# One attention and mixture kernel on one core: scores and values issued back to back, and the last two tiles interleaved

## The chip, the core and the metric

The kernel runs on one core of a Trainium2 chip. A core has a matrix engine (TensorE, "PE" in the profile; its weight loads are shown apart as "PEld"), VectorE (DVE), ScalarE (ACT), GpSimd (POOL) and SyncE (SP), which issues the transfers (DMAs) here. Each engine works through its own queue in order, and engines wait for one another by semaphores. In this kernel TensorE writes its results to an accumulation memory (PSUM), from which VectorE and ScalarE copy them out. The metric is the time of one execution in microseconds (us), as the median of several runs; lower is better. Beside it stands one profiled execution, whose "span" goes from its first to its last instruction.

## The reference

Two sandwich blocks on 4 sequences of 512 tokens, 1024 wide, all in float32. Attention is causal with 32 heads of 32 columns that share 8 key and value heads; the second block is a dense layer with eight low-rank experts, two of them chosen for each token.

```python
x = x + _layernorm(attn(_layernorm(x), w_qkv, b_qkv, w_o, b_o))
x = x + _layernorm(ffn(_layernorm(x), gate_w, base_w, base_b, lora_A, lora_B))

# attn
qkv = x @ w_qkv.T + b_qkv
...
scores = jnp.einsum('bhqd,bhkd->bhqk', rope(q), rope(k)) / math.sqrt(HEAD_DIM)
attn = jax.nn.softmax(jnp.where(causal, scores, -1e20), axis=-1)
out = jnp.einsum('bhqk,bhkd->bhqd', attn, v)
return out.reshape(bs, seq_len, d_model) @ w_o.T + b_o

# ffn
weights, selected = jax.lax.top_k(x @ gate_w.T, 2)
w_full = jnp.sum(jax.nn.one_hot(selected, E) * jax.nn.softmax(weights)[..., None], axis=2)
low = jnp.einsum('bsd,erd->ebsr', x, lora_A)
return x @ base_w.T + base_b + 2.0 * jnp.einsum('ebsr,eor,bse->bso', low, lora_B, w_full)
```

## The kernel before

The 2048 tokens are 16 tiles of 128. They are worked on in the order of `line`: tiles 0 to 11, then 13, 14, 15, and tile 12 last. Tile t is the i-th of its sequence (i = t mod 4), and its queries see i + 1 blocks of 128 keys. So tile 12, the first of its sequence, has the shortest attention.

For each tile: x is loaded (`load_x`), normalised (`Norm`: statistics on VectorE, the root on GpSimd, the scaling on VectorE) and transposed on TensorE (`transposes`, tiles pt_xn, copied out to T_xn). `project` multiplies it by the query, key and value weights in eight steps of 128 rows (acc_kv, acc_q); `rotated` applies the rotary angles; TensorE turns keys and queries (pt_k, pt_q) into kT and qT.

Attention runs in groups. A group holds one to four of the eight columns of heads in a tile, and four heads ("quadrants") for each column. There are 2, 4, 8 or 8 groups for i = 0, 1, 2, 3: 88 in all. A group's stages:

- `scores`: matmuls that use only 32 rows of the array, four side by side, one for each quadrant (sc, 32*128 in the profile). There is one buffer for sc in PSUM, and four smaller ones for everything else that TensorE writes.
- `softmax`: VectorE adds the causal mask on the diagonal block (L1019) and takes the maxima of all four quadrants (L1029). Then, quadrant by quadrant, ScalarE takes exponentials and sums (L982), VectorE the reciprocals (L991), GpSimd scales (L996): pr.
- `turn`: TensorE transposes a quadrant's pr (pt_p, L1043); VectorE or ScalarE copies it out (prT). pr and prT share eight buffers.
- `values`: matmuls that use only 32 columns of the array (av, L1066, 128*32 in the profile), copied out to aT.

`attention_out` multiplies aT by the output weights (acc_o), adds the bias (L740), normalises, adds into y on GpSimd (`add_half`, L401), and normalises again to w. `ffn` transposes w (pt_h, copied to T_h), multiplies it by the gate and low-rank weights (acc_gl), picks the experts (`gate`), transposes the weighted low part (pt_low), multiplies by the base and low-rank weights (acc_f), normalises, adds into y on GpSimd, and stores the two halves.

The order of all instructions is made by a planner in the program, `Order`, before anything runs. It holds an estimated duration for each operation, a clock for each engine, and Tasks that carry the time at which something is finished. `Order.run` gives each of VectorE, ScalarE, GpSimd and SP the most urgent ready operation; `copy` can go to either of two engines. `Order.tensor` gives TensorE its next step from lanes: the scores, the transposes of each tile, the transposes and values of the groups (all these are "urgent", in that order), and then the dense products. A step that has been ready for SAFE (0.6 us) is taken first, otherwise one that is just ready, and otherwise the planner lets its clock go on. What the planner writes down is each engine's order; the chip then runs at its own pace, with semaphore waits.

A group's scores need the queries, the keys, the exponentials of the group before (which frees sc) and the transposes of the group before that. Its values need all four prT.

Of the kernel before, what the change touches and what calls it, by code (L numbers as in the profile page):

```python
# [16 lines left out]
P = 128  # L17
# [13 lines left out]
FILL = 0.3  # L31
SAFE = 0.6
# [44 lines left out]
class Step:  # L77


    def __init__(self, us, issue, needs=(), bank=False):  # L80
        self.us, self.issue, self.needs = us, issue, list(needs)
        self.bank = bank
        self.done = Task()


class Order:
# [14 lines left out]
    def _go_on(self, chain, task, at):  # L101
        self.at = at
# [74 lines left out]
    def tensor(self, urgent, dense):  # L177


        while any(urgent) or any(dense):  # L180
            self.run(self.now)
            known, safe = [], None
            dense = [lane for lane in dense if lane]
            urgent = [lane for lane in urgent if lane]
            for lane in urgent + sorted(dense, key=lambda lane: lane[0].bank):
                at = self._ready(lane[0])
                if at is not None:
                    known.append((at, lane))
                    if at + SAFE <= self.now:
                        safe = lane  # L190
                        break
            if safe is None:
                lane = next((lane for at, lane in known if at <= self.now), None)
                if lane is None:
                    later = [at for at, _ in known]
                    what = self._next()
                    if what is not None:
                        later.append(max(what[0], self.now + 1e-6))
                    if not later:
                        raise RuntimeError("TensorE's work cannot go on")  # L200
                    self.now = min(later)
                    continue
                safe = lane
            step = safe.pop(0)
            if step.bank:
                heapq.heappop(self.banks.free)
            step.issue()
            self.now += step.us
            step.done.finish(self.now + FILL)
        self.run(float("inf"))  # L210
# [3 lines left out]
def kernel(  # L214
# [130 lines left out]
    class Norm:  # L345
# [6 lines left out]
        def half(self, src, h):  # L352
            if self.stats is None:
                self.stats = small.tile([P, NH, 6], F32, tag="stats", name=f"stats_{self.name}")
            cols = slice(h * 512, (h + 1) * 512)
            yield dve(
                0.69,
                self.urgent,
                lambda: nc.vector.bn_stats(out=self.stats[:, h, :], in_=src()[:, cols]),  # L359
            )  # L360

        def scale(self):
            name = self.name

            def aggr():
                self.mv = small.tile([P, 2], F32, tag="mv", name=f"mv_{name}")
                nc.vector.bn_aggr(out=self.mv, in_=self.stats)

            def eps():
                self.veps = small.tile([P, 1], F32, tag="veps", name=f"veps_{name}")  # L370
                nc.vector.tensor_scalar_add(self.veps, self.mv[:, 1:2], EPS)  # L371

            def root():
                self.rstd = small.tile([P, 1], F32, tag="rstd", name=f"rstd_{name}")
                nc.gpsimd.tensor_tensor(out=self.rstd, in0=self.veps, in1=neg_half, op=ALU.pow)  # L375
# [20 lines left out]
    def add_half(y, z, h, urgent):  # L396
        cols = slice(h * 512, (h + 1) * 512)
        yield pool(
            1.3,
            urgent,  # L400
            lambda: nc.gpsimd.tensor_tensor(  # L401
                out=y()[:, cols], in0=y()[:, cols], in1=z()[:, cols], op=ALU.add
            ),
        )
# [119 lines left out]
    class Job:  # L524


        def __init__(self, tok, name, has_k=True, has_q=True):
            self.tok, self.name, self.has_k, self.has_q = tok, name, has_k, has_q
            self.issued, self.in_x = Task(), Task()
# [13 lines left out]
    def load_x(job):  # L543
# [5 lines left out]
        def issue():  # L549
            job.issued.finish(order.at)  # L550
            job.xn = xpool.tile([P, D], F32, tag="xa", name=f"xa_{job.name}")
            nc.sync.dma_start(out=job.xn, in_=x[job.tok.t * P : (job.tok.t + 1) * P, :])

        yield sp(P * D * 4 / 1024 / RATE, issue)
        yield LANDS
        job.in_x.finish(order.at)
# [16 lines left out]
    def qkv(job, has_k, has_q):  # L573
# [6 lines left out]
        def normed():  # L580
            yield job.in_x
            for h in range(NH):
                yield from norm.half(lambda: job.xn, h)
# [129 lines left out]
    def attention_out(tok):  # L713
# [31 lines left out]
        def sum_half(h):  # L745
            yield from norms[0].apply(w, w, h)
            yield from add_half(lambda: tok.y, w, h, 1)
# [71 lines left out]
    def ffn(tok):  # L819
# [67 lines left out]
        def out_half(h):  # L887
            yield from norm.apply(lambda: tok.w, lambda: tok.w, h)
            yield from add_half(lambda: tok.y, lambda: tok.w, h, 2)
# [55 lines left out]
    class Group:  # L945
        def __init__(self, tok, at, n):
            self.tok, self.seq, self.at, self.n = tok, tok.seq, at, n
            self.kt = at // GROUP
            self.name = f"{tok.t}_{at}"
            self.exps, self.normed = [Task() for _ in range(QUADS)], [Task() for _ in range(QUADS)]  # L950
# [3 lines left out]
    def scores(g):  # L954
# [15 lines left out]
        nmax = small.tile([P, QUADS, GROUP], F32, tag="nmax", name=f"nmax_{g.name}")  # L970
        total = small.tile([P, QUADS, GROUP], F32, tag="total", name=f"total_{g.name}")
        rtot = small.tile([P, QUADS, GROUP], F32, tag="rtot", name=f"rtot_{g.name}")
# [34 lines left out]
        def softmax():  # L1007
# [5 lines left out]
            if not seq.left[g.kt]:  # L1013
                kT_slots.give(order.at)
            diag = sc4[:, :, :, i * P : n]
            yield dve(
                0.15 + g.n * 0.54,
                1,
                lambda: nc.vector.tensor_tensor(  # L1019
                    out=diag,  # L1020
                    in0=diag,
                    in1=cmask.unsqueeze(1).unsqueeze(1).to_broadcast([P, QUADS, g.n, P]),
                    op=ALU.add,
                ),
            )
            yield dve(
                0.15 + g.n * n * 0.0042,
                1,
                lambda: nc.vector.tensor_reduce(  # L1029
                    nmax[:, :, : g.n], sc4, AX.X, ALU.max, negate=True  # L1030
                ),
            )
            for r in range(QUADS):
                start(quadrant(r), order.at)
# [104 lines left out]
    for tok in line:  # L1139
        n = min(GROUP, NQ // (tok.i + 1))  # L1140
        for at in range(0, ND, n):
            g = Group(tok, at, n)
            blocks = n * (tok.i + 1)
            needs = [tok.has_q[g.kt]] + [tok.seq.has_k[i] for i in range(tok.i + 1)]
            if groups:
                needs += groups[-1].exps
            if len(groups) > 1:
                needs += [s.done for s in groups[-2].turned]
            g.scored = Step(0.2 + 0.218 * blocks, partial(scores, g), needs)
            g.turned = [  # L1150
                Step(0.109 * blocks, partial(turn, g, r), [g.normed[r]], bank=True)
                for r in range(QUADS)
            ]
            needs = g.has_prT + [tok.seq.has_v[i] for i in range(tok.i + 1)] + [tok.aT_taken]
            g.valued = Step(0.2 + 0.218 * blocks, partial(values, g), needs, bank=True)
            score_lane.append(g.scored)
            value_lane += g.turned + [g.valued]
            groups.append(g)
# [14 lines left out]
    order.tensor([score_lane, *turn_lanes, value_lane], dense_lanes)  # L1173
# [77 lines left out]
```

## Time and profile before

| | us |
|---|---|
| median of 3 runs (lowest and highest) | 1246.99 (1245.8, 1247.3) |
| the profiled execution | 1245.69 |
| its span | 1243.8 |
| first matmul starts | 7.60 |
| last product on TensorE starts (two passes) | 1233.92 |
| time on the chain that ended last: acc_f, acc_q, acc_o | 20%, 18%, 17% of the span |
| the same: transposes pt_p, scores sc, values av | 12%, 7%, 6% |

How to read it: the profile gives, for each engine, the time in which it was busy, and for each group of instructions the line, the engine, the tiles written and read, the count, the busy time and the mean of one. Float32 products take two passes through the array, so one step of `project` shows as two matmuls. Matmuls overlap in the pipeline, and their ends are modelled; the distance from one start to the next is what they really cost. "idle before" is the time in which the engine did nothing before such instructions, and behind the arrow stands what ended most of it. Granted clock over the span: 0.998.

### The profile page before, as it was taken

Reading aid. Unit: us, or ns where it says so; the run is one execution under the profiler, and the core shown is the slowest. Engines: PE = TensorE matmul, PEld = TensorE weight load, DVE = VectorE, ACT = ScalarE, POOL = GpSimd, SP = SyncE. Lnnn points to the kernel's source line nnn. Section 1 sums busy time; section 2 is a strip of 40 time slices with the busy share of each in tenths; the row PEclk is TensorE's granted clock in tenths of the full one; section 3 lists DMA queues with packets and bytes.
Section 4 is the critical chain, followed back from the end, with each engine's and each line's share of the span. In section 5 each row is a group of like instructions: output and inputs, shape, how many; then the busy total and the mean of one; then the engine's idle time right before and its main releaser. Section 6 shows DMA issues by size and latency. Waiting matters only on the chain.

```text
span 1243.8 us, 19733 instructions
## 1 busy us (share of the span) xinstructions
PE 1221.4 (98%) x7416; PEld 653.2 (53%) x7416; DVE 803.5 (65%) x1655; ACT 428.4 (34%) x1354; POOL 452.2 (36%) x700
## 2 busy tenths in 40 slices
PE   7999999999999999999999999999999999999997
PEld 3555555555555555555545555555555555555543
DVE  3656668666566675776555667677657766757553
ACT  0344344444212443344313323344333333343400
POOL 1343425325332443335242423434324334343332
PEclk9999999999999999999999999999999999999999
DMA  9700001001010100101010101002001010010010
GB/s 353 303 1 18 1 1 52 1 1 52 1 51 1 52 1 17 36 1 34 2 51 1 52 1 52 2 1 69 1 1 51 1 52 1 1 51 1 1 34 34
DMA packets 16205, 44.67 MB, mean 36 GB/s; under 512 B 2160, under 2 KB 3184, under 8 KB 16112
## 3 DMA queue, kind: packets, MB, share of 16 engines
q1 hardware_dynamic: 16112, 43.42, 10.0%
q8 instruction: 59, 0.97, 0.3%
q14 instruction: 34, 0.28, 0.1%
HBM read 35.03 MB, written 8.39 MB: 35 GB/s over the span
## 4 chain that ended last, share of the span: by engine, by line
PE 96%; DVE 1%; issue 1%; POOL 1%; DMA 0%; ACT 0%; POOLq 0%; ACTq 0%
PE acc_f L442 20%; PE acc_q L442 18%; PE acc_o L442 17%; PE pt_p L1043 12%; PE acc_kv L442 9%; PE sc L962 7%; PE av L1066 6%; PE acc_gl L442 3%; PE pt_xn L417 1%; PE pt_h L417 1%; PE pt_q L666 1%; POOL y L401 0%; PE pt_k L635 0%; DVE stats L359 0%; DMA xa<-in_x_dram 0%
## 5 line engine op out<-in xcount | busy, mean ns | idle before, releaser
L996 POOL TENSOR_SCALAR pr<-pr,rtot 128x256 f32<-128x256 f32 (+3 forms) x512 | 280.4, 562 | 377.0 <-DVE rtot L991 324.5
L982 ACT ACTIVATE pr<-sc,nmax 128x256 f32<-128x256 f32 (+3 forms) x512 | 262.9, 533 | 146.7 <-DVE nmax L1029 133.0
L442 PE MATMUL acc_f<-wbase_sb,T_h 128*128 128x512 f32 x512 | 241.0, 598 | 0.0
L442 PE MATMUL acc_o<-wo_sb,aT 128*128 128x512 f32 x512 | 237.8, 598 | 0.4 <-ACT aT L280 0.4
L442 PE MATMUL acc_q<-wqkv_sb,T_xn 128*128 128x512 f32 x480 | 225.3, 597 | 1.0 <-DMA wqkv_sb<-in_w_qkv_dram 0.9
L280 ACT COPY prT<-pt_p 128x512 f32<-128x512 f32 (+1 forms) x189 | 102.2, 549 | 304.5 <-PE pt_p L1043 303.7
L1043 PEld LDWEIGHTS pt_p<-ident,pr 128*128 128x128 f32 x1280 | 148.7, 141 | 108.3 <-issue 81.6
L1029 DVE TENSOR_REDUCE nmax<-sc 128x4 f32<-128x1536 f32 (+3 forms) x88 | 184.2, 2093 | 1.4
L1043 PE MATMUL pt_p<-ident,pr 128*128 128x128 f32 x1280 | 181.2, 275 | 1.1 <-POOL pr L996 1.1
L281 DVE COPY prT<-pt_p 128x512 f32<-128x512 f32 (+1 forms) x163 | 104.4, 641 | 90.8 <-PE pt_p L1043 88.7
L442 PEld LDWEIGHTS acc_o<-wo_sb,aT 128*128 128x128 f32 x512 | 90.6, 190 | 88.8 <-issue 87.6
L442 PEld LDWEIGHTS acc_f<-wbase_sb,T_h 128*128 128x128 f32 x512 | 89.2, 190 | 79.6 <-issue 78.9
L442 PEld LDWEIGHTS acc_q<-wqkv_sb,T_xn 128*128 128x128 f32 x480 | 84.1, 190 | 79.5 <-issue 75.1
L442 PE MATMUL acc_kv<-wqkv_sb,T_xn 128*128 128x512 f32 x256 | 121.6, 601 | 0.6 <-DVE T_xn L281 0.6
L1019 DVE TENSOR_TENSOR sc<-sc,cmask 128x512 f32<-128x512 f32 (+2 forms) x88 | 82.5, 938 | 48.5 <-PE sc L962 47.7
L982 ACT ACTIVATION_READ_ACCUMULATOR pr<-sc,nmax 128x1 f32 x512 | 108.4, 212 | 0.0
L401 POOL TENSOR_TENSOR y<-y,w 128x512 f32<-128x512 f32 x64 | 84.3, 1326 | 64.8 <-DVE w L386 53.3
L375 POOL TENSOR_TENSOR rstd<-veps,neg_half 128x1 f32<-128x1 f32 x64 | 35.3, 553 | 178.1 <-DVE veps L371 153.0
L1066 PEld LDWEIGHTS av<-prT,v 128*32 128x32 f32 x2560 | 65.2, 109 | 63.9 <-issue 34.7
L962 PE MATMUL sc<-kT,qT 32*128 32x384 f32 (+3 forms) x1024 | 93.9, 464 | 0.0
L1066 PE MATMUL av<-prT,v 128*32 128x128 f32 x2560 | 90.0, 276 | 1.0 <-DVE veps L371 0.6
L489 POOL TENSOR_TENSOR raw_q<-raw_q,rope_sb 128x512 f32<-128x512 f32 x32 | 41.0, 1281 | 121.1 <-DVE turn_q L478 104.6
(81 smaller groups left out, 903.7 us busy)
## 6 DMA issues: line engine op xcount, KB each, us to landing
xa<-in_x_dram SPq DMA_DIRECT2D x16, 512.0 KB, 3.5
y<-in_x_dram SPq DMA_DIRECT2D x16, 512.0 KB, 3.6
out_dram<-y SPq DMA_DIRECT2D x32, 256.0 KB, 2.0
wqkv_sb<-in_w_qkv_dram SPq DMA_DIRECT2D x8, 512.0 KB, 9.5
wo_sb<-in_w_o_dram SPq DMA_DIRECT2D x8, 512.0 KB, 8.3
wbase_sb<-in_w_base_dram SPq DMA_DIRECT2D x8, 512.0 KB, 10.4
wqkv_sb<-in_w_qkv_dram SPq DMA_DIRECT2D x8, 256.0 KB, 6.4
bqkv_sb<-in_b_qkv_dram SPq DMA_DIRECT2D x1, 768.0 KB, 7.8
```

The costliest lines, as they stand in the source:

```text
L280: act=(0.15 + n * 0.00085, lambda: nc.scalar.copy(out(), in_())),
L281: dve=(0.15 + n * 0.00105, lambda: nc.vector.tensor_copy(out(), in_())),
L401: lambda: nc.gpsimd.tensor_tensor(out=y()[:, cols], in0=y()[:, cols], in1=z()[:, cols], op=ALU.add),
L442: nc.tensor.matmul(acc[0][:, :n], lhsT=lhsT()[:, c, :] if c < ND else more[0](), rhs=w_sb[:, c, at : at + n] if c < ND else more[1][:, at ...
L489: lambda: nc.gpsimd.tensor_tensor(out=raw3, in0=raw3, in1=cos, op=ALU.mult),
L962: nc.tensor.matmul(sc[:, r, c * n : (c + 1) * n], lhsT=tok.qT[g.kt][rows, (g.at + c) % GROUP, :], rhs=seq.kT[g.kt][rows, :n], start=True, ...
L982: lambda: nc.scalar.activation(pr[:, c * n : (c + 1) * n], sc4[:, r, c, :], AF.Exp, bias=nmax[:, r, c : c + 1], accum_out=total[:, r, c : ...
L996: lambda: nc.gpsimd.tensor_scalar(pr[:, c * n : (c + 1) * n], pr[:, c * n : (c + 1) * n], rtot[:, r, c : c + 1], 1.0, ALU.mult, ALU.mult,),
L1019: lambda: nc.vector.tensor_tensor(out=diag, in0=diag, in1=cmask.unsqueeze(1).unsqueeze(1).to_broadcast([P, QUADS, g.n, P]), op=ALU.add,),
L1029: lambda: nc.vector.tensor_reduce(nmax[:, :, : g.n], sc4, AX.X, ALU.max, negate=True),
L1043: nc.tensor.transpose(pt[:, j, :], g.pr[r][:, j * P : (j + 1) * P], ident)
L1066: nc.tensor.matmul(av[r * HD : (r + 1) * HD, c, :], lhsT=g.seq.v[j][:, head * HD : (head + 1) * HD], rhs=g.prT[r][:, c * (i + 1) + j, :], ...
```

## The change

It has seven parts.

1. *Pairs.* Scores and values are marked `tiled`. When a score step is chosen and the next value step is ready, both are issued together. A score step that is ready is put last if the next value step will come (all it needs but the prT of the group has been given a time) and is not ready yet; a value step is put last likewise if the next score step will come. `soon` names the needs that don't count for "will come": the exponentials of the group before for scores, prT for values.
2. *Costs in the planner.* A tiled step costs 0.4 us (TILING) on top of its work when alone, and 0.55 (PAIRED) for a pair; before it was 0.2 each.
3. *Interleaving.* The groups of the last two tiles (15 and 12) no longer follow tile by tile: tile 12's first group comes before the last two of tile 15.
4. *Maxima in two parts* for the last two tiles: mask and maximum for two quadrants, then for the other two.
5. *The last tile's additions into y* may go to VectorE or GpSimd.
6. *x is loaded in two halves*, and the statistics of a half start when that half is there.
7. *More small buffers*: 4 instead of 2 for a norm's statistics, 3 instead of 2 for the sums of the softmax.

```diff
+TILING = 0.4
+PAIRED = 0.55
...
-    def __init__(self, us, issue, needs=(), bank=False):
-        self.us, self.issue, self.needs = us, issue, list(needs)
-        self.bank = bank
+    def __init__(self, us, issue, needs=(), bank=False, soon=()):
+        self.us, self.issue, self.needs = us, issue, list(needs) + list(soon)
+        self.tiled = False
+        self.bank, self.soon = bank, soon
...
+    def _is_ready(self, step):
+        at = self._ready(step)
+        return at is not None and at <= self.now
+
+    def _comes(self, step):
+
+        return all(t.at is not None for t in step.needs if t not in step.soon)
+
+    def _choice(self, scores, values, lanes):
+
+        later, ready, last = [], [], []
+        score = scores[0] if scores else None
+
+
+        value = values[0] if values and values[0].tiled else None
+        waiting = []
+        if score is not None and value is not None:
+            if self._comes(score):
+                waiting.append(values)
+            if self._comes(value) and not self._is_ready(value):
+                waiting.append(scores)
+        for lane in lanes:
+            at = self._ready(lane[0])
+            if at is None:
+                continue
+            later.append(at)
+            if at <= self.now:
+                if any(lane is w for w in waiting):
+                    last.append(lane)
+                elif at + SAFE <= self.now:
+                    return lane, None
+                else:
+                    ready.append(lane)
+        if ready or last:
+            return (ready + last)[0], None
...
+            steps = [lane.pop(0)]
+            us = steps[0].us + TILING * steps[0].tiled
+            if lane is scores and values and values[0].tiled and self._is_ready(values[0]):
+                steps.append(values.pop(0))
+                us = steps[0].us + steps[1].us + PAIRED
+            for step in steps:
+                self._take(step)
+            self.now += us
...
-                self.stats = small.tile([P, NH, 6], F32, tag="stats", name=f"stats_{self.name}")
+                self.stats = small.tile([P, NH, 6], F32, tag="stats", bufs=4, name=f"stats_{self.name}")
...
-    def add_half(y, z, h, urgent):
+    def add_half(y, z, h, urgent, either=False):
+
         cols = slice(h * 512, (h + 1) * 512)
...
+        def issue(engine):
+            engine.tensor_tensor(out=y()[:, cols], in0=y()[:, cols], in1=z()[:, cols], op=ALU.add)
+
+        on = {"pool": (1.3, partial(issue, nc.gpsimd))}
+        if either:
+            on["dve"] = (0.7, partial(issue, nc.vector))
+        yield Op(urgent, **on)
...
+        for h in range(NH):
+            cols = slice(h * 512, (h + 1) * 512)
+            yield sp(
+                P * 512 * 4 / 1024 / RATE,
+                lambda: nc.sync.dma_start(out=job.xn[:, cols], in_=x[rows, cols]),
+            )
+            start(lands(h), order.at)
+        job.issued.finish(order.at)
...
+            self.parts = 2 if self.tok in line[-2:] else 1
...
+            q = QUADS // g.parts
+            for r0 in range(0, QUADS, q):
+                some = slice(r0, r0 + q)
+                diag = sc4[:, some, :, i * P : n]
+                yield dve(
+                    0.15 + q * g.n * 0.135,
...
+                        nmax[:, some, : g.n], sc4[:, some], AX.X, ALU.max, negate=True
+                    ),
+                )
+                for r in range(r0, r0 + q):
+                    start(quadrant(r), order.at)
...
-            g.scored = Step(0.2 + 0.218 * blocks, partial(scores, g), needs)
...
+        groups += [Group(tok, at, n) for at in range(0, ND, n)]
+
+    *groups, g0, g1 = groups
+    groups.insert(len(groups) - 0, g1)
+    groups.insert(len(groups) - 3, g0)
+    for k, g in enumerate(groups):
...
+        soon = groups[k - 1].exps if k else []
+        if k > 1:
+            needs += [s.done for s in groups[k - 2].turned]
+        g.scored = Step(0.218 * blocks, partial(scores, g), needs, soon=soon)
...
+        needs = [tok.seq.has_v[i] for i in range(tok.i + 1)] + [tok.aT_taken]
+        g.valued = Step(0.218 * blocks, partial(values, g), needs, bank=True, soon=g.has_prT)
+        g.scored.tiled = g.valued.tiled = True
...
-    order.tensor([score_lane, *turn_lanes, value_lane], dense_lanes)
+    order.tensor(score_lane, turn_lanes, value_lane, dense_lanes)
```

## The prediction

> **What bounds the kernel now.** I read the page first: who is busy, and the chain that ended last.
>
> ```profile
> PE 1221.4 (98%) x7416; PEld 653.2 (53%) x7416; DVE 803.5 (65%) x1655; ACT 428.4 (34%) x1354; POOL 452.2 (36%) x700
> ...
> PE 96%; DVE 1%; issue 1%; POOL 1%; DMA 0%; ACT 0%; POOLq 0%; ACTq 0%
> ```
>
> TensorE is the bound nearly everywhere, so an edit pays if it takes time out of TensorE's own row, or a wait out of it. Next, TensorE's timeline over one group (start, length, count; a start is the reliable number):
>
> ```profile
> 1108.77 1.02 PE L442 MATMUL acc_q<-wqkv_sb,T_xn_12q 128*128 128x512 f32 x2
> 1109.72 1.14 PE L962 MATMUL sc<-kT,qT 32*128 32x512 f32 x8
> 1110.79 1.09 PE L1043 MATMUL pt_p<-ident,pr 128*128 128x128 f32 x8
> 1111.72 1.88 PE L442 MATMUL acc_q<-wqkv_sb,T_xn_12q 128*128 128x512 f32 x4
> 1113.54 1.08 PE L1066 MATMUL av<-prT,v 128*32 128x128 f32 x32
> 1114.55 2.84 PE L442 MATMUL acc_q<-wqkv_sb,T_xn_12q 128*128 128x512 f32 x6
> 1117.22 0.60 PE L666 MATMUL pt_q<-ident,raw_q 128*128 128x128 f32 x4
> ```
>
> Elsewhere a full-array pass of 512 columns starts every 0.429 us and a transpose every 0.109 (median start to start in the trace). Here 2 passes should take 0.86 and the scores start after 0.95: going into a tiled form costs 0.09. The last score pass starts 0.517 before the next full-array one, not 0.429: coming out costs 0.09. Then eight transposes take 0.93 and not 0.87, six dense passes 2.67 and not 2.57: the first weight load after a tiled block is not hidden, 0.056 before transposes, 0.104 before dense passes. All 88 score blocks and 88 value blocks of the trace show these values within 0.01.
>
> Summed so, TensorE's row is full-array passes 1013.9, tiled blocks 169.8, 176 entries 16.4, first loads 14.5, waits 12. The waits are the start (about 4), some 2 in the middle, and the end (the bracket gives the idle time and its releaser):
>
> ```profile
> 1144.86 0.66 PE L1043 MATMUL pt_p<-ident,pr 128*128 128x128 f32 x4 [1.08 <-POOL pr L996]
> ...
> 1197.48 1.19 PE L442 MATMUL acc_gl<-wgl_sb,T_h 128*128 128x136 f32 x8 [0.94 <-DVE T_h L281]
> ...
> 1199.90 1.19 PE L442 MATMUL acc_gl<-wgl_sb,T_h 128*128 128x136 f32 x8 [0.78 <-DVE veps L371]
> ```
>
> By starts these are 1.25, 1.1 and 0.94 late; two value blocks (at 1145.4 and 1179.7) take 2.16 and 2.37 where others take 1.01, and 0.2 is unhidden loads: 6.0 in all.
>
> **The change, part by part**, against the profiled execution's 1245.69 us (span 1243.8). The median of the runs shown, 1246.99, is 1.3 higher, which I add at the end.
>
> *Pairing.* In the new TensorE order 68 score blocks are followed at once by a value block and 2 the other way round; in the old order none is. Entries fall from 176 to 106. First loads were 96 before dense passes and 80 before transposes (14.5); now 15 and 91: 15 x 0.104 + 91 x 0.056 = 6.7, so 7.8 less. Changes of form were 352; now 106 in, 106 out and 70 between two tiled forms. The price of the last kind, x, is in no row. From below it is 0 (no drain); from above 0.29, out through the full array and in again (0.09 + 0.09 + 0.104). Every change that the trace has costs 0.088 to 0.094, whatever stands on either side, so I take x = 0.093: 70 fewer changes x 0.093 = 6.5. Sum: -14.3; with x = 0 it is -20.8, with 0.29 -0.5.
>
> The Trainium skill, "TensorEngine Tiling (Array Packing)", Tiling Modes, says that changing the tiling mode, not just the tile, drains the engine. That speaks against x = 0, but gives no price.
>
> *What the pairing delays.* A score step now waits for the next values, so softmax has more TensorE work over it: from a score block to its first transpose the old order has at least 5.85 us of TensorE work (which did not stall), the new one 7.9 or more except at two places at the end. Between two scores the least was 5.3 and is, but for the same places, 8.0. The added cover costs nothing in the middle; were it gone, each stall would be paid in full. One first transpose of a token loses its cover (0.44, the same that cost 0.84 at 112 us in the old run), one stall of 0.78 (at 422) goes. I set the middle to 0.
>
> *The interleaving.* The order is now: tile 15's groups 0 to 5, tile 12's first, tile 15's groups 6 and 7, tile 12's last. Tile 15's output projection needs group 6, which now comes one group later. Between tile 14's last output-projection pass and the transposes of its normalised sum (pt_h) TensorE has three tiled blocks (3.4 with entries), 20 transposes (2.2) and loads (0.2): 5.75 us. The same chain, on VectorE in the old run:
>
> ```profile
> 1134.04 0.69 DVE L740 TENSOR_TENSOR w<-acc_o,bo_sb 128x512 f32<-128x512 f32 x1 [0.17 <-PE acc_o L442]
> ...
> 1143.98 2.29 DVE L1019 TENSOR_TENSOR sc<-sc,cmask 128x2048 f32<-128x2048 f32 x1
> 1146.31 2.29 DVE L1029 TENSOR_REDUCE nmax<-sc 128x16 f32<-128x2048 f32 x1
> ...
> 1151.24 1.00 DVE L386 TENSOR_SCALAR w<-y,mv,rstd 128x512 f32<-128x512 f32 x2 [0.67 <-POOL rstd L375]
> ```
>
> Bias at 1134.0, first half normalised at 1151.8: 17.8 us, then hidden under tile 15's projection. In the new VectorE queue the same operations again have a group's maxima and both mask and maxima of tile 12's first group among them. In two parts these are 1024 columns: mask 1.23 (its 1024 row), maximum 2.29 - 2 x 0.53 = 1.22 (0.53 from the 2048 and 1536 rows). Walked through: bias 0.7, two maxima and a mask 2.9, statistics and reciprocals 1.5, probability copies waiting for transposes 1.8, normalise 0.5, two copies behind the scores 1.8, four halves of mask and maximum 4.9, normalise, add (POOL 1.3) and statistics 2.9, root and normalise 1.2: 18.2, near the row. I take the row: TensorE waits 17.8 + 0.15 (hand-over) - 5.75 = 12.2. Lower bound: the chain with the softmax out of its way took 10.6 (at 1196.1 to 1206.7): 4.8. Upper, by the walk with slips: 16. All that follows on TensorE is late by as much.
>
> A wait of that length also touches the clock. The windows view has
>
> ```profile
> 1239.60:1243.80 4.20, 0.00 (x0) 0.00 (x0) 0.00 (x0) 0.00 (x0) 1.30 (x2) 0.50 0.33 125
> ```
>
> (the 0.50 is the granted clock): half clock 4.7 us after the last matmul. And after the idle start the first eight transposes took 1.71 instead of 0.87 and the first sixteen passes 7.6 instead of 6.9: 1.6 lost. In the new hole I see two idle stretches, near 4 and 8 us, about a value block; one is over 4.7: +1.6 (0 if the clock stays).
>
> The Trainium skill, "TensorE: Matmul & The Clock Gate", Part 1, has the clock halved after one idle window of about 3.4 us; by that both stretches would do it, which would put a further 1.6 on the sum. No run here shows an idle of 4 us followed by work.
>
> *End.* The old end waits go: tile 12's last values have 1.8 us of projection after their transposes, and the gate's products 2.2 and 1.8 after pt_h, where the old waits were about 1.1 after the transposes' end. -6.0. Splitting adds 2 VectorE instructions to each of 10 groups, hidden but for the walk above.
>
> *Tail.* Both last sums go to VectorE (two of 0.7, like the 0.725 row of L494) from GpSimd (2.71). VectorE's four then end at about 1240.0 and not 1240.9: -0.9.
>
> *Start.* x in halves lets the first statistics (0.65) begin before the second half lands, but the fifth query chunk came at 21.8 by DMA and its bytes are the same; only the second token's normalisation gains: -0.5 (0 to -0.65). Twice as many x loads queue on SP; from load to use there is idle SP time in every token. More small buffers only remove waits.
>
> Sum: -14.3 + 12.2 + 1.6 - 6.0 - 0.9 - 0.5 = -7.9: 1237.8, as a median **1239.1**.
>
> **Rivals.** *A, the switch between tiled forms is dear* (slower): at each of the 70 pairs x = 0.29, since the two forms split the array in different directions. For it: no such pair is in the trace. Against: all changes cost the same. -7.9 + 13.8 = +5.9: 1252.9. It decides from x = 0.206 on (7.9 / 70 above 0.093). *B, the hole is short*: the chain runs almost bare, 4.8, and the clock stays: -7.9 - 7.4 - 1.6: 1230.1. For it: maxima in two parts and smaller softmax pieces; against it the queue order. *C, tiled to tiled is free*: x = 0: 1232.6. *D, the pairs are not made*: the order shows 70 of 88, so I give it nothing.
>
> **How the numbers follow.** Forecast 0.55, A 0.16, B 0.15, C 0.14. The forecast's own width is the hole's +-3 and the clock. The range 1231 to 1249 leaves out A's upper part and B's lower. What this kernel's measurement can tell from no change is 0.2%, 2.5 us. Faster: 0.48 of the forecast, B and C, 0.01 of A: 0.78. Same: 0.06 + 0.02 = 0.08. Slower: 0.13 of A, 0.01 of the forecast: 0.14.
>
> **What would show it.** In the new profile: the start of av after the last sc pass (0.52 for 512 columns if x = 0.09, 0.43 if free, 0.7 if dear); a hole of 10 to 14 us before pt_h of tile 14, some 100 us ahead of the end, with transposes of 0.21 after it; no waits over 0.3 behind it; last sums on DVE. Waits in the middle, or a hole of under 6 us, would make the prediction wrong.

## The result, and the profile after

The changed kernel takes 1246.62 us (median of 14 runs, 1245.2 to 1247.96), the kernel before, beside it, 1246.29 (14 runs): ratio 1.0001, 95% interval 0.9993 to 1.001. The forecast gain of 7.9 us did not come. The profiled execution took 1246.57 with a span of 1244.7 (before: 1245.69 and 1243.8), at a granted clock of 0.991 instead of 0.998.

The page first: TensorE's share, the chain that ended last, and two of the costliest groups (busy time and mean ns, then idle time before them and what ended it).

```profile
PE 1212.1 (97%) x7416; PEld 659.6 (53%) x7416; DVE 807.8 (65%) x1678; ACT 430.2 (35%) x1355; POOL 450.6 (36%) x696
...
PE 96%; DVE 2%; ACT 0%; POOL 0%; DMA 0%; issue 0%; POOLq 0%; SPq 0%; ACTq 0%
...
L1103 PE MATMUL pt_p<-ident,pr 128*128 128x128 f32 x1280 | 178.9, 277 | 13.5 <-POOL pr L1053 13.0
L1089 DVE TENSOR_REDUCE nmax<-sc 128x4 f32<-128x1536 f32 (+5 forms) x98 | 185.6, 1894 | 9.7 <-ACT pr L1039 8.7
```

The same two groups on the page of before:

```profile
L1029 DVE TENSOR_REDUCE nmax<-sc 128x4 f32<-128x1536 f32 (+3 forms) x88 | 184.2, 2093 | 1.4
L1043 PE MATMUL pt_p<-ident,pr 128*128 128x128 f32 x1280 | 181.2, 275 | 1.1 <-POOL pr L996 1.1
```

TensorE is less busy than before (1221.4), in a span that is not shorter. New idle time stands ahead of the transposes of probabilities: 13.5 us instead of 1.1, nearly all ended by GpSimd's scaling. And VectorE's maxima now wait for ScalarE's exponentials, which should come after them (9.7 us instead of 1.4). TensorE's timeline shows where (start, length, in brackets the idle time before):

```profile
1108.04 1.14 PE L1019 MATMUL sc<-kT,qT 32*128 32x512 f32 x8
1109.11 1.08 PE L1126 MATMUL av<-prT,v 128*32 128x128 f32 x32
...
1113.74 1.08 PE L1126 MATMUL av<-prT,v 128*32 128x128 f32 x32
1119.28 2.09 PE L1103 MATMUL pt_p<-ident,pr 128*128 128x128 f32 x8 [4.46 <-POOL pr L1053]
1121.30 2.09 PE L1019 MATMUL sc<-kT,qT 32*128 32x128 f32 x32
1123.32 1.44 PE L1103 MATMUL pt_p<-ident,pr 128*128 128x128 f32 x8
...
1134.87 1.17 PE L1103 MATMUL pt_p<-ident,pr 128*128 128x128 f32 x3 [8.11 <-POOL pr L1053]
...
1136.81 1.09 PE L465 MATMUL pt_h<-ident,w 128*128 128x128 f32 x4
```

The first two rows are a pair, and cost what was forecast: from the start of the scores to the start of the values 1.07, of which 0.517 after the start of the last score pass. In all 68 such pairs the values start as long after the last score pass as full-array work did before, within 0.002 us (0.517 to 0.518 for 512 columns, 0.200 for 128, where full-array passes take 0.429 and 0.109), and in the two the other way round the scores start 0.202 to 0.203 after the last value pass, as full-array work does.

The rest is what I call the hole: two idle stretches with slow work between and after them. I measure every wait by laying TensorE's order out at the durations of the prediction (0.429 a pass, 0.109 a transpose and so on), as an axis, and seeing how far the real starts fall behind it. In the kernel before, they are 11.3 us behind at 24 us, 14.2 at 1072 and 20.3 at the end. In the changed kernel they are 12.0 behind at 24 us, 16.3 at 1114, 35.75 at the first base product of tile 14 (start 1143.80) and 36.5 at the end. In differences:

| | predicted | measured |
|---|---|---|
| TensorE's work, entries, switches, first loads | -14.3 | -14.3 |
| start and middle | -0.5 | +2.1 |
| hole (wait and clock) | +12.2 + 1.6 | +19.5 |
| end waits (6.1 before, 0.7 after) | -6.0 | -5.4 |
| tail | -0.9 | -0.9 |
| sum, against a span that is 0.9 longer | -7.9 | +1.0 |

The first row is the two orders laid out at those durations. Laid out at the median of every start-to-start distance in the traces, it is -14.5.

The windows view of the same stretch (length, then busy time of PE, PEld, DVE, ACT, POOL; the last three columns are clock, DMA share and GB/s) shows the clock:

```profile
1114.80:1119.20 4.40, 0.02 (x3) 0.00 (x0) 2.62 (x5) 1.88 (x6) 0.67 (x1) 0.78 0.00 0
1119.20:1126.70 7.50, 7.23 (x80) 5.51 (x80) 5.36 (x12) 1.28 (x4) 4.02 (x6) 0.67 0.00 0
1126.70:1134.80 8.10, 0.07 (x1) 0.00 (x0) 5.53 (x8) 4.37 (x24) 1.62 (x3) 0.76 0.00 0
1134.80:1142.00 7.20, 6.73 (x29) 4.11 (x30) 4.11 (x11) 2.29 (x11) 6.09 (x17) 0.56 0.01 3
1142.00:1150.00 8.00, 8.00 (x51) 4.48 (x53) 5.57 (x19) 4.26 (x11) 2.77 (x4) 1.00 0.00 0
```

Both idle stretches take the clock to half, and the work behind each runs at it: the scores at 1121.30 take 2.02 to the next start, where such a block takes 1.10 elsewhere. The DVE timeline, and then the ACT timeline, show why the chain was longer than the 17.8 us of the old row:

```profile
1115.70 0.43 DVE L1079 TENSOR_TENSOR sc<-sc,cmask 128x256 f32<-128x256 f32 x1
1117.04 1.23 DVE L1089 TENSOR_REDUCE nmax<-sc 128x2 f32<-128x1024 f32 x1 [0.91 <-ACT pr L1039]
...
1128.08 1.23 DVE L1079 TENSOR_TENSOR sc<-sc,cmask 128x1024 f32<-128x1024 f32 x1
1130.60 1.22 DVE L1089 TENSOR_REDUCE nmax<-sc 128x8 f32<-128x1024 f32 x1 [1.28 <-ACT pr L1039]
```

```profile
1116.23 0.69 ACT L1039 ACTIVATE pr<-sc,nmax 128x512 f32<-128x512 f32 x1 [1.08 <-DVE sc L1079]
...
1129.41 0.37 ACT L1039 ACTIVATE pr<-sc,nmax 128x128 f32<-128x128 f32 x1 [2.34 <-DVE sc L1079]
```

The exponentials of the first two quadrants wait for the mask of the other two (released by sc L1079, not by their own maximum), and the maximum of the other two waits for exponentials of the first. Nothing in the mathematics asks for it: both parts lie in one tile, sc.

### The profile page after: what moved, and what is told of

Its sections match the earlier page's. It is cut to its first block, busy times and chain, and to the rows that moved or that the text cites. A ratio compares the mean times of both kernels' runs of the same rounds, so it can differ in the third digit from the quotient of the medians.

```text
span 1244.7 us, 19839 instructions
## 1 busy us (share of the span) xinstructions
PE 1212.1 (97%) x7416; PEld 659.6 (53%) x7416; DVE 807.8 (65%) x1678; ACT 430.2 (35%) x1355; POOL 450.6 (36%) x696
## 4 chain that ended last, share of the span: by engine, by line
PE 96%; DVE 2%; ACT 0%; POOL 0%; DMA 0%; issue 0%; POOLq 0%; SPq 0%; ACTq 0%
PE acc_f L490 20%; PE acc_o L490 18%; PE acc_q L490 17%; PE pt_p L1103 12%; PE acc_kv L490 9%; PE sc L1019 7%; PE av L1126 6%; PE acc_gl L490 2%; PE pt_h L465 1%; PE pt_q L721 1%; PE pt_xn L465 1%; DVE nmax L1089 0%; PE pt_k L690 0%; ACT pr L1039 0%; DMA xa<-in_x_dram 0%; DVE stats L405 0%
## 5 line engine op out<-in xcount | busy, mean ns | idle before, releaser
L1053 POOL TENSOR_SCALAR pr<-pr,rtot 128x256 f32<-128x256 f32 (+3 forms) x512 | 283.9, 572 | 405.0 <-DVE rtot L1048 369.7
L490 PE MATMUL acc_f<-wbase_sb,T_h 128*128 128x512 f32 x512 | 236.0, 593 | 0.2 <-ACT prT L326 0.2
L490 PE MATMUL acc_o<-wo_sb,aT 128*128 128x512 f32 x512 | 233.2, 593 | 0.0
L1103 PE MATMUL pt_p<-ident,pr 128*128 128x128 f32 x1280 | 178.9, 277 | 13.5 <-POOL pr L1053 13.0
L1089 DVE TENSOR_REDUCE nmax<-sc 128x4 f32<-128x1536 f32 (+5 forms) x98 | 185.6, 1894 | 9.7 <-ACT pr L1039 8.7
L327 DVE COPY prT<-pt_p 128x512 f32<-128x512 f32 (+1 forms) x159 | 101.8, 642 | 64.3 <-PE pt_p L1103 62.3
L490 PE MATMUL acc_kv<-wqkv_sb,T_xn 128*128 128x512 f32 x256 | 118.0, 598 | 0.7 <-DVE veps L417 0.3
L1079 DVE TENSOR_TENSOR sc<-sc,cmask 128x512 f32<-128x512 f32 (+3 forms) x98 | 83.8, 855 | 18.7 <-PE sc L1019 18.0
L447 POOL TENSOR_TENSOR y<-y,w 128x512 f32<-128x512 f32 x60 | 79.3, 1334 | 39.2 <-DVE w L432 38.6
L1048 DVE RECIPROCAL rtot<-total 128x1 f32<-128x1 f32 (+2 forms) x352 | 51.9, 156 | 52.8 <-ACT pr L1039 50.7
```

The costliest lines, as they stand in the source:

```text
L327: dve=(0.15 + n * 0.00105, lambda: nc.vector.tensor_copy(out(), in_())),
L447: engine.tensor_tensor(out=y()[:, cols], in0=y()[:, cols], in1=z()[:, cols], op=ALU.add)
L490: nc.tensor.matmul(acc[0][:, :n], lhsT=lhsT()[:, c, :] if c < ND else more[0](), rhs=w_sb[:, c, at : at + n] if c < ND else more[1][:, at ...
L1048: yield dve(0.17, 1, lambda: nc.vector.reciprocal(rtot[:, r, : g.n], total[:, r, : g.n]))
L1053: lambda: nc.gpsimd.tensor_scalar(pr[:, c * n : (c + 1) * n], pr[:, c * n : (c + 1) * n], rtot[:, r, c : c + 1], 1.0, ALU.mult, ALU.mult,),
L1079: lambda: nc.vector.tensor_tensor(out=diag, in0=diag, in1=cmask.unsqueeze(1).unsqueeze(1).to_broadcast([P, q, g.n, P]), op=ALU.add,),
```

## The experiments

Two questions. What brings the hole: the pairs or the interleaving? And why is it 19.5 us and not 13.8? Below, "the parts" are the maxima in two parts (the fourth part of the change), and a chain is "bare" where TensorE has no work of its own beside it and waits.

### What each part does alone

*pairs_alone*: the changed kernel without interleaving and parts.

```diff
-            self.parts = 2 if self.tok in line[-2:] else 1
+            self.parts = 1
...
-    *groups, g0, g1 = groups
-    groups.insert(len(groups) - 0, g1)
-    groups.insert(len(groups) - 3, g0)
```

> Pairs kept; the interleaving and the maxima in two parts undone (tile 15's groups, then tile 12's, one maximum each). Theory 1 (the pairs set attention back, so that little dense work is left about 100 us before the end): TensorE's row is 14.2 us shorter than before as in the changed kernel, but the order has covers of 2.1 to 3.1 us over softmax chains of some 9 us near 1110 us, and none at all under the two last transposes of normalised sums (bare chain 10.6 us each): some 10 to 12 plus 20 us of waits, time 1255 to 1268. Theory 2 (the interleaving makes the hole): without it only the row counts, 1232 to 1237.

Measured 1258.36 (ratio to the kernel before 1.0098, 95% interval 1.0083 to 1.0113): theory 1's range. TensorE's timeline has a hole of 11.5 us near 1115 and two bare chains of tiles 15's and 12's sums:

```profile
1183.12 1.08 PE L465 MATMUL pt_h<-ident,w 128*128 128x128 f32 x4 [8.88 <-DVE w L432]
...
1228.64 1.97 PE L465 MATMUL pt_h<-ident,w 128*128 128x128 f32 x8 [7.91 <-DVE w L432]
```

*all_but_pairs*: the two conditions that hold a lane back and issue two steps together are made false.

```diff
-        if score is not None and value is not None:
+        if False:
...
-            if lane is scores and values and values[0].tiled and self._is_ready(values[0]):
+            if False:
```

> Scores and values are never held back for one another nor issued together; the interleaving, the parts and the rest stay. TensorE's row is 0.6 us shorter than before. Theory 1 (the pairs bring the hole): a smaller hole stays, since the order still has 2.6, 3.6 and 6.6 us of work over the chains at the interleaved groups; it is 6 to 10 us, less the 6.1 us of end waits of before, so 1245 to 1251. Theory 2 (the interleaving alone makes the hole of 19.5 us): 1257 to 1262.

Measured 1261.49 (1.0123, 1.0106 to 1.014), by the number theory 2's range, but for a reason of neither theory: 8.8 us of it are a stall in the middle, which the changed kernel does not have.

```profile
361.00 1.09 PE L721 MATMUL pt_q<-ident,raw_q 128*128 128x128 f32 x4 [5.43 <-DVE raw_q L542]
```

The rotated queries are late because a product of theirs stands in GpSimd's queue behind the scaling of probabilities, as the POOL timeline has it, though VectorE had written raw_q by 356.3:

```profile
356.57 2.06 POOL L1053 TENSOR_SCALAR pr<-pr,rtot 128x256 f32<-128x256 f32 x4 [0.20 <-DVE rtot L1048]
358.60 1.25 POOL L537 TENSOR_TENSOR raw_q<-raw_q,rope_sb 128x512 f32<-128x512 f32 x1
```

The order had nothing else for TensorE there. Idle time, half clock and late transposes come to 8.8. Without it the run would be at 1252.7. Its hole near 1150 is 12 to 13 us: neither the 6 to 10 of theory 1 nor the 19.5 of theory 2.

*small_parts_alone*: the diffs of pairs_alone and of all_but_pairs together, so that the halves of x, the additions, the buffers and the planner's cost of a tiled step are left.

> No pairs, no interleaving, one maximum for each group; x in halves, the last additions on either engine, more small buffers and the planner's new cost of a tiled step stay. TensorE's row is 0.3 us shorter than before; tail 0.9 less; start and middle together 2 more, as in the changed kernel: 1245.5 to 1248. Rival (these parts alone move the time by more than 2 us, for instance by the stall of 8.8 us at 361 us that the run without pairs has): 1249 to 1256.

Measured 1255.37 (1.0068, 1.0052 to 1.0083): the rival, by the same stall (5.42 us idle at 360, 9.7 in all). Less that, the median is 1245.7 and the profiled execution (1257.53) 1247.8, both in the range expected. So the small changes are worth nothing that shows, and their order without pairs has a stall which the pairs' order happens not to have. What any part "is worth" depends on the order that the planner makes around it.

*halves_no_interleave* leaves out the interleaving alone:

```diff
-    *groups, g0, g1 = groups
-    groups.insert(len(groups) - 0, g1)
-    groups.insert(len(groups) - 3, g0)
```

> Pairs and maxima in two parts kept, the interleaving undone. Theory 1 (the parts, not the interleaving, remove the waits of 12 and 10 us at the end that pairs alone have; the interleaving then only places the hole): the order has 11 to 13 us of work under the three last transposes of sums and covers of 2.1 and 0.1 us near 1100 us; a hole of 8 to 13 us, 1240 to 1246. Theory 2 (the interleaving is what removes those waits): 1254 to 1258, as with pairs alone.

*interleave_no_halves* leaves out the parts alone:

```diff
-            self.parts = 2 if self.tok in line[-2:] else 1
+            self.parts = 1
```

> Pairs and interleaving kept, one maximum for each group. Theory 1 (the parts remove the waits at the end): covers of 1.3 us at 1149 and 0 at 1182 stay as with pairs alone, 1252 to 1260. Theory 2 (the interleaving removes them): within 3 us of the changed kernel.

Measured 1251.34 (1.0038, 1.0024 to 1.0052) and 1263.83 (1.0139, 1.0121 to 1.0156). The second shows the wait of theory 1, since without the parts the bare chain under the last pt_h stays (7.9 us idle), but lies 3.8 above its range; two of its four executions took 1261.8 and two 1265.8. The first lies between the theories: a hole of 16 us near 1120, then 9 us of small waits from 1181 on. With pairs, the four corners are: neither 1258.4, parts 1251.3, interleaving 1263.8, both 1246.6. The parts gain in either case; the interleaving gains 4.7 only with the parts and costs 5.5 without.

That answers the first question: either brings a hole. With pairs alone it is 11.5 us, with the interleaving and the parts but no pairs 12 to 13, and with none of them (small_parts_alone) there is none: its waits from 1100 to 1165 add up to 2.

### Does pairing set attention back?

*pairs_to_76*: steps are no longer held back for one another in the last 12 groups, and no pair is made there; interleaving and parts are undone as in pairs_alone.

```diff
-        if score is not None and value is not None:
+        if score is not None and value is not None and score.pair:
...
+        g.scored.pair = g.valued.pair = k < 76
```

> Pairs are made only for the first 76 of the 88 groups (a score step is no longer held back for values after that, nor a value step for scores); the interleaving and the maxima in two parts are undone. TensorE's row is 12.2 us shorter than before, 2.1 less than with all pairs. Theory 1 (holding scores back near the end is what puts attention behind the dense work; given 12 unpaired groups it catches up): the order has 10 us or more of work under the last transposes and three value blocks with 0.09 us over their copies, 1.1 us each, as before: no hole, time 1246.2 - 12.2 + 2.1 (start and middle as in the changed kernel) - 0.9 (tail) = 1235, 1233 to 1238. Rival (68 groups of pairing have already set it back): a hole of 8 us or more near 1110 us, 1243 or more.

Measured **1234.98** (ratio 0.9906, 0.9891 to 0.9921): theory 1, whose sum was 1235, and a version that beats both kernels. It differs from pairs_alone in the last 12 groups' order and is 23.4 us faster. The order says why. When the scores of the 84th group are issued, the dense work still to come (0.429 for a pass of 512 columns, 0.116 for one of 136) is 92.2 us in the kernel before, 81.1 in the changed one, 79.4 with pairs alone and 93.1 here. A scores step held back for values lets the planner give its place to dense work; over 76 groups that costs little, but the last groups' chains then lie bare. Here they don't, as TensorE's timeline shows at the place of the hole:

```profile
1113.14 7.13 PE L490 MATMUL acc_o<-wo_sb,aT 128*128 128x512 f32 x16
1120.11 0.60 PE L721 MATMUL pt_q<-ident,raw_q 128*128 128x128 f32 x4
1120.64 1.14 PE L1019 MATMUL sc<-kT,qT 32*128 32x512 f32 x8
1121.71 1.97 PE L1103 MATMUL pt_p<-ident,pr 128*128 128x128 f32 x16
...
1135.40 1.06 PE L1126 MATMUL av<-prT,v 128*32 128x128 f32 x26 [0.33 <-ACT prT L326]
```

The largest wait left of the old kind is 1.25 us (behind the value block); the end waits of before, 6.4 us in all, are back as expected.

*to76_interleaved*, *to76_halves* and *to76_halves_split*: the same limit, with both end edits, with the parts alone, and with the parts and the split tile of the next section. All have the diff of pairs_to_76 just shown; the last two leave the three lines of the interleaving out.

> As the changed kernel, with pairs for the first 76 groups only. Theory (the interleaving has a price of its own: it puts the chain of tile 14's normalised sum and two groups' softmax side by side over 2.6 to 6.9 us of TensorE work): a hole of 7 to 12 us stays near 1110 us, 4 us of end waits go, 1238 to 1243. Rival (the interleaving costs only because attention is behind): 1231 to 1235.

> Pairs for the first 76 groups, no interleaving, but the maxima in two parts kept for the last two tiles. Theory (with attention no longer behind, the parts shorten the softmax of the last groups and give the planner room to put work between the transposes and the values): TensorE's order has one value block with 0.09 us over its copy where the run without parts has three, so two waits of 0.85 and 1.25 us go: 1232 to 1234. Rival (the parts' waits for one another through the shared tile cost as much): 1235 to 1237.

> The run with pairs for 76 groups and parts, its score tile split in two for the last two tiles; every engine's order is the same. Theory (the split is worth its 3.6 us only where TensorE waits for a softmax chain; here none waits): within 0.7 us of the run without the split. Rival (the false wait also costs elsewhere): 1 to 3 us less.

Measured 1244.53 (0.9984, 0.9975 to 0.9993), 1245.16 (0.9986, 0.9977 to 0.9994) and 1240.76 (0.995, 0.9938 to 0.9963). The first misses its range by a little: with 98.2 us of dense work left it still has a hole, of some 14 us with 17 us at half clock, so the interleaved order makes one of its own. In the changed kernel, then, ending the pairs early gains only 2.1. The two others miss widely. With parts and no interleaving there is no hole near 1115, but 17 us of late starts from 1149 on, around the last two pt_h and the gate's products, where pairs_to_76 has 6.4. The split takes 4.4 back, but not by the false wait alone: in its profile the clock is at half for 3.4 us there, in that of to76_halves for 17. So my theory that the parts also help an order without bare chains falls: they helped one with them (pairs_alone) and cost 10 us here. What the planner's order changes there I did not trace to the bottom.

### Why 19.5 us and not 13.8?

*split_sc*: in the last two tiles each half of the scores has a tile of its own, in the same place; the order of every engine is that of the changed kernel.

```diff
+        if g.parts == 2 and len(sc_pool) == 1:
+            sc_ctx.close()
+            sc_pool.append(sc_ctx.enter_context(tc.tile_pool(name="ps_sc2", bufs=2, space=PSUM)))
...
+            scs = [
+                sc_pool[1].tile([P, 2, 512], F32, tag="sc", name=f"sc{h}_{g.name}") for h in range(2)
+            ]
```

> For the last two tiles the scores of a group lie in two tiles of two quadrants each, in the place of the one; every engine's order is that of the changed kernel. Theory (the two parts wait for one another only because they share a tile: the exponentials of the first part for the mask of the second, the maximum of the second for the exponentials of the first): each chain in the hole loses 1 to 2 us, the hole goes from 19.5 to 15.5 to 17.5, time 2 to 4 us under the changed kernel, 1242.5 to 1244.5. Rival (VectorE's queue sets the chain): within 0.5 us of the changed kernel.

Measured 1242.97 (0.9975, 0.9965 to 0.9984), 3.65 under the changed kernel: the theory. The DVE timeline has the second maximum right behind its mask, and nothing released by ScalarE:

```profile
1126.70 1.22 DVE L1089 TENSOR_TENSOR sc<-sc,cmask 128x1024 f32<-128x1024 f32 x1
1127.95 1.22 DVE L1099 TENSOR_REDUCE nmax<-sc 128x8 f32<-128x1024 f32 x1
```

TensorE's two idle times are 3.43 and 6.09 (4.46 and 8.11 before the split).

*warm*: transposes of the identity ahead of the two waits, to keep TensorE busy.

```diff
+        if r == 0:
+            for _ in range({"15_5": 36, "12_0": 56}.get(g.name, 0)):
+                nc.tensor.transpose(pt[:, 0, :], ident, ident)
```

> 36 and 56 transposes of the identity are put ahead of the two groups of transposes at which TensorE waits 4.5 and 8.1 us in the hole, so that it isn't idle; they are overwritten. Theory (both idle stretches bring the clock to half, and work at half clock lengthens the hole): no drop of the granted clock there, scores of 1.1 us instead of 2.0, the hole goes from 19.5 to 14.5 to 16.5, time 3 to 5 us under the changed kernel, 1241.5 to 1243.5. Rival (the chains on the other engines set all of it): 0 to 1 us less.

Measured 1244.76 (0.9988, 0.9979 to 0.9997), 1.9 less: between theory and rival. The first drop is gone, the second is not. The 56 transposes ended too early, and TensorE's timeline has

```profile
1124.51 6.33 PE L1104 MATMUL pt_p<-ident 128*128 128x128 f32 x56
1132.68 1.02 PE L1106 MATMUL pt_p<-ident,pr 128*128 128x128 f32 x3 [1.84 <-POOL pr L1053]
1134.24 0.48 PE L1106 MATMUL pt_p<-ident,pr 128*128 128x128 f32 x1 [0.54 <-POOL pr L1053]
1134.62 1.09 PE L465 MATMUL pt_h<-ident,w 128*128 128x128 f32 x4
1135.63 2.09 PE L1019 MATMUL sc<-kT,qT 32*128 32x512 f32 x8
```

The trace's record of the clock has half clock from 1133.78 for 6.8 us, after the idle time of 1.84 and three transposes, just as the idle time of 0.54 begins: the block at 1135.63 shows it by its length.

*split_warm*: both, with other numbers of transposes.

```diff
-            for _ in range({"15_5": 36, "12_0": 56}.get(g.name, 0)):
+            for _ in range({"15_5": 30, "12_0": 54}.get(g.name, 0)):
```

> The split of the score tile and the transposes of the identity (30 and 54) together, TensorE idle for about 2 us in all in the hole. Theory (both costs are real and apart; in the run with the transposes alone the clock still dropped once, at the second wait, because they ended 1.8 us too early): split 3.6 less, first drop 1.9 less, second drop up to 3 less: 1238 to 1240 if no drop is left, 1241 if the second is. Rival (the same microseconds are counted twice, the chain sets both): 1242 to 1243, as with the split alone.

Measured 1239.62 (0.9943, 0.9928 to 0.9958), 7.0 under the changed kernel. Its windows, over the hole, stay at full clock:

```profile
1114.60:1118.10 3.50, 3.50 (x36) 3.26 (x30) 3.29 (x7) 2.55 (x8) 0.70 (x2) 1.00 0.00 0
1118.10:1123.70 5.60, 4.99 (x81) 3.62 (x80) 4.63 (x10) 0.61 (x2) 3.94 (x5) 1.00 0.00 0
1123.70:1129.90 6.20, 6.18 (x56) 5.88 (x54) 5.52 (x8) 4.41 (x24) 1.68 (x3) 1.00 0.01 3
1129.90:1137.00 7.10, 6.41 (x45) 4.71 (x46) 5.49 (x14) 3.76 (x14) 6.24 (x16) 1.00 0.00 1
```

The size of the hole in these four kernels, as the time from the value block ahead of it (1113.74 in the changed kernel) to the first base product behind it (1143.80), less the 10.5 us of work on the axis: 19.5 changed, 18.8 warm, 16.65 split, 12.7 both. So the false wait is 2.9, the clock, with that wait gone, 3.9, and 12.7 is left, which is the bare 12.2 of the prediction within 0.5. The chain itself agrees: from the bias to the first pt_h it takes 18.2 us in split_warm (1113.74 to 1131.91), against the 17.95 predicted.

## Why the prediction was wrong, and where it was right

- *Pairing, -14.3*: right within 0.2 us. The switch between the two tiled forms costs the same as any change of form here, within 0.002 us, and first loads fell as counted. Rivals A (0.29) and C (free) are both dead by that number alone, and D (not made) too.
- *Interleaving, hole +12.2*: the place and the kind of chain were right, the size was not. The step that failed is "I take the row: TensorE waits 17.8 + 0.15 (hand-over) - 5.75 = 12.2". That row is a chain of the old kernel, with one maximum for each group and under full-clock work. In the new kernel the two parts wait for one another in the shared score tile, which no term had: bias to pt_h is 23.0 us (1113.85 to 1136.81) instead of 17.95. The split measured 2.9 for that wait. Without it, and with the clock kept up, the row holds (18.2).
- *Clock, +1.6*: the second failed step, measured at 3.9. I let one idle stretch of the two drop the clock, because the one row that I had, half clock 4.7 us after the last matmul, made 4 us seem safe. Both dropped it. The Trainium skill, "TensorE: Matmul & The Clock Gate", Part 1, has the clock fall after one idle window of some 3.4 us, and the sum by it would have been 1.6 worse. That was the better guide than my row; yet the runs go further, since the clock dropped in warm with no single idle time above 1.84, and in small_parts_alone with none above 0.92.
- *The prediction's outcome as a sum*: these two steps make 5.7 of the 8.8 us by which -7.9 missed +0.9. Start and middle make 2.6: a wait of 0.59 at 347 us and two of 0.64 and 0.43 at 233 and 235, where I had allowed 0.44, and a start that I credited with -0.5. Those waits come with the pairs' order: between 220 and 360 us the starts fall back by 2.1 to 2.5 us in all eleven profiles with pairs, and by 0.3 or less in the three without (before, all_but_pairs, small_parts_alone). The start can't be read that closely: at 24 us the profiles with the new start are 10.8 to 12.4 us behind the axis, the one before 11.3.
- *End waits, -6.0, and tail, -0.9*: right within 0.6. But the end waits were paid for: pairs_to_76 has them back and is 11.6 us faster than the changed kernel.
- *Rival B, a short hole*: wrong in the other direction; "maxima in two parts" spoke for it, and the parts, in one shared tile, lengthened the chain.
- *What the pairing delays*: I read the longer cover of the middle (7.9 us and more) as harmless, and but for the 2 us of waits just named it was. What I missed is its other side: the same holding back uses up dense work, 11.1 us of it by the 84th group (92.2 against 81.1), and the end has to do without it. I took the covers at the end from the order, so their effect was in the 5.75; I did not see that the pairing had a share in making them small, and that it could be stopped in time. That pairing in the last 12 groups costs an order without the end edits 23.4 us is shown by pairs_to_76 against pairs_alone. In the changed kernel it is not the whole cause of the hole: the interleaving brings one without pairs (all_but_pairs) and with pairs ended early (to76_interleaved). What each end edit does for a given order of the planner is only partly shown.

## What to carry to other kernels

When a planner is made to hold one kind of work back, count near the place where the last of that work is issued how much filling work is left (too little is a warning; enough is no promise, as to76_interleaved shows); a gain spread over the whole kernel is easily given back in its last tenth, and switching the new rule off there may keep nearly all of it (here 12.2 of 14.3 us). An operation cut in two only runs as two if its tiles are two: look at what releases each half in the profile. And a predicted wait on the bounding engine can have a second price, the work behind it at half clock; count it for each idle stretch.

## What the runs showed of the hardware

- A switch between matmuls that use 32 rows and matmuls that use 32 columns of the array costs the same as one from or to the full array, in 70 of 70 cases: 0.088 to 0.094 us more than a full-array pass of as many columns takes (compared at 128 and 512 columns).
- Within a run, the clock's changes to half and back lie multiples of 3.41 us apart, and it fell after less idle time than I had thought: in the changed kernel 2.4 us after TensorE stopped (1114.8 to 1117.25), in warm after 1.84 and three transposes. With 0.42 and 0.58 us idle (split_warm) it did not fall. It stayed at half for 3.4 to 17 us.
- Several short waits can do it. In small_parts_alone the clock is at half from 1208.04 for 6.8 us, with no longer idle time ahead of it than these:

```profile
1205.66 0.63 PE L465 MATMUL pt_h<-ident,w 128*128 128x128 f32 x4 [0.92 <-DVE w L432]
1207.07 1.29 PE L490 MATMUL acc_gl<-wgl_sb,T_h 128*128 128x136 f32 x8 [0.78 <-DVE T_h L327]
1208.16 1.06 PE L465 MATMUL pt_h<-ident,w 128*128 128x128 f32 x4
```

The same two waits in pairs_to_76 (0.91 and 0.78, at 1185.90 and 1187.31) left it at full, so it also matters when they fall. In all 38 drops on record in these traces TensorE had been busy, by the modelled ends, for at most 0.53 of the 3.41 us before; but one such stretch of 0.41 (interleave_no_halves, up to 1225.3) did not drop it, so the share alone is not shown to be the rule.
